# Layer 0 of a four-layer network: the second expert stage in four groups of one batch, where two batches shared a group

## The chip, the cores and the metric

The kernel runs on one core of one Trainium2 chip. Its engines are TensorE (PE; its weight loads are shown apart as PEld), VectorE (DVE), ScalarE (ACT), GpSimd (POOL) and SyncE (SP), which here only starts transfers. Each works through its own list of instructions in order and waits for the others by semaphores. The metric is the device time of one execution in microseconds; the median of three runs is 3132.94 us (3131.44 to 3135.03).

## The reference, cut to what matters

The activations `x` are 4 batches of 1024 tokens of 128 channels here. Each layer is a "macaron": half a feed-forward network, an attention, and half the feed-forward network again, each on a layer norm of `x`, each added to `x`:

```
x = x + 0.5 * _L0_ffn_ref(_layernorm(x), ...)      # n = 0 in the kernel
x = x + _L0_attn_ref(_layernorm(x), ...)           # "middle"
x = x + 0.5 * _L0_ffn_ref(_layernorm(x), ...)      # n = 1 in the kernel: the change is here
x = x + 0.5 * _L1_ffn_ref(_layernorm(x), ...)      # "last"
...
```

Layer 0's feed-forward network is a mixture of experts. A router picks 2 of 8 experts for every token and weighs them by a softmax of the two logits; each expert is `gelu(x @ w1.T + b1) @ w2.T + b2` with 512 hidden units:

```
top_vals, top_idx = jax.lax.top_k(logits, K)
probs = jax.nn.softmax(top_vals, axis=-1)
for e in range(E):
    w = jnp.sum(jnp.where(top_idx == e, probs, 0.0), axis=-1)
    h = jax.nn.gelu(jnp.einsum('td,fd->tf', xf, w1[e]) + b1[e], approximate=False)
    y = jnp.einsum('tf,df->td', h, w2[e]) + b2[e]
    out = out + w[:, None] * y
```

Layer 0's attention is over the 16 heads within one token (a 16 x 16 table for every token, 8 channels a head), so a batch's attention needs only that batch's `x`, and so does everything else in the layer. Layers 1 to 3 follow; nothing of them is changed.

## The kernel before, in words

`x` stays in SBUF with channels as partitions, one tile of 128 x 1024 for each batch (`self.X`). A token tile is 128 tokens, so a batch has 8.

Layer 0 is a set of tasks, each a Python generator that writes instructions and yields a planned cost from time to time:

- `route{n}{b}` (`route`, L290 to L428) for expert stage n and a group of batches named by its first, b. It norms the batches, writes their rows to DRAM (L307), takes the top two of the logits, counts the tokens of each expert and gives every token-and-expert pair a slot. Slots come in blocks of 128 of one expert. Its results are tables: `g_source` (which row fills a slot, L416), `g_target` (where a slot's result goes, L419), `g_expert` (each block's expert, L389), `g_p1`, `g_p2` (the weights). Most of it is short VectorE instructions.
- `experts{n}{b}` (`experts`, L430 on), over the group's blocks. For each: SP loads the expert's whole weights `e_w` (L450, a ring of 5 buffers, 578 KB each); POOL gathers 128 rows into `e_xg` (L452); PE transposes them (L456) and VectorE copies them to `e_x` (L458); 4 matmuls up with Gelu on ACT into `e_h` (L466); 4 matmuls down; VectorE adds the bias into `e_y` (L477); POOL scatters the rows to DRAM, `res` (L478). Three blocks are in flight, in different steps.
- `combine{n}{b}` (`combine`, L488 on) for one batch: SP reads the two results of each token back, `c_y` (L503), ACT and VectorE weigh and add them (L508, L509), PE transposes, VectorE adds half of it to `x` (L251).
- `middle{b}` (`l0_attn`, L517 on): layer 0's attention of a batch, 8 token tiles. A tile is mostly four long VectorE instructions of about 2.3 us (two products, L544 and L561, and two sums, L546 and L563), and ends with the product at L564. After four tiles, `x` gets the result (L588); the second L588 ends the task.
- `last{b}` (`l1_ffn`): layer 1's first half feed-forward network of a batch.

How many blocks a group has is fixed by its size, whatever the tokens choose: `blocks_of(tiles)` is (256 x tiles + 8 x 127) // 128, the slots that are needed if every expert's last block is nearly empty. That is 23 for one batch (8 tiles) and 39 for two (16 tiles).

`lanes` (its planner) writes the tasks' instructions down. It keeps a planned clock for every lane and always goes on with the lane whose clock is least; a task starts once the tasks that it names as its predecessors are written. Layer 0 has four lanes: all experts in turn, all combines in turn, a lane with the first stage's routing, the four attentions and the four `last`, and a lane with the second stage's routing. The Tile framework then gives each engine its order, from that order of writing.

The tables of a routing exist once for each mark (`bufs=1`):

```
one = lambda shape, tag, dtype=F32: self.t(wp, shape, tag + mark, dtype, bufs=1)
```

so that a routing with the same mark as an earlier one must wait for the earlier one's last reader. In the kernel before, the second stage has the groups (0, 1), (2,) and (3,), with the marks `_0`, `_1` and `_2`. The routing of (0, 1), `route10`, names `middle0`, `middle1` and `combine03` as its predecessors.

Of the kernel before, what the change touches and what calls it, by code (L numbers as in the profile page):

```python
# [18 lines left out]
B, S, D = 4, 1024, 128  # L19
# [188 lines left out]
class Macaron:  # L208
# [1040 lines left out]
    def layer0(self, moe, m, right, enter, ffn):  # L1249
        m["wqkvc"] = self.centered(m["wqkv"], 3 * D)  # L1250
        pa, pf = enter(right, "l0a"), enter(right, "l1f0")
        side, main = self.side, self.main

        def more(route):
            attn = lambda b, *after: (f"middle{b}", after, lambda: self.l0_attn(side, pa, m, b))
            last = lambda b, ps: (f"last{b}", (f"combine1{b}",), ffn(pf, ps, b))
            return (
                [
                    route(0, (0,), ps=main), route(0, (1,)), route(0, (2, 3)),
                    *[attn(b, f"combine0{b}") for b in range(B)],  # L1260
                    last(0, side), last(1, side), last(2, side), last(3, main),
                ],
                [route(1, (0, 1), "middle0", "middle1", "combine03"), route(1, (2,), "middle2"), route(1, (3,), "middle3")],
            )


        groups = [(0,), (1,), (2, 3)], [(0, 1), (2,), (3,)]
        marks = {(0, (0,)): "_1", (0, (1,)): "_2", (0, (2, 3)): "_0", (1, (0, 1)): "_0", (1, (2,)): "_1", (1, (3,)): "_2"}
        self.macaron("l0", moe, AF.Gelu, groups, marks, more)

    def layer2(self, moe, m, right, enter, ffn):
# [118 lines left out]
```

## Time and profile before

| | us |
|---|---|
| median of three runs | 3132.94 (3131.44 to 3135.03) |
| the profiled execution | 3239.76 |
| its span | 3237.5 |
| layer 0, up to the end of `last3` | 928 |

| share of the span busy | PE | PEld | VectorE | ACT | POOL |
|---|---|---|---|---|---|
| whole kernel | 85% | 49% | 57% | 50% | 25% |

The profiled execution is the one that all lines of the profile come from; it takes longer than the timed runs. Layer 0 lies in the first twelve of the page's 40 slices (each 81 us). In a line of a group or of the timeline, L and a number is the line of the kernel, then come the operation and "out<-in" by the program's names; "[0.30 <-PE bank L456]" is idle time of the engine before that instruction, and who ended it. A table of stretches gives the busy time of each engine in each stretch with its number of instructions, then the granted TensorE clock (1.00 is full), the mean busy share of the DMA engines and the GB/s that they moved.

In the trace of before, the second stage's gathers start at 493.9 us (`experts10`), about 656 us (`experts12`) and 783.4 us (`experts13`); the first stage's last scatter is issued at 377.1 us. The attentions end at 305.5, 421.7, 572.8 and 733.8 us.

### The profile page before, as it was taken

The numbers are of one execution on the slowest core, as the hardware profiler recorded it, in microseconds if no ns is written. First come the engines' busy times: TensorE is split into PE (matmuls) and PEld (weight loads), VectorE is DVE, ScalarE is ACT, GpSimd is POOL, SyncE is SP. The second block draws the span as 40 slices with busy tenths as digits, with TensorE's granted clock in tenths as the row PEclk, the third lists the DMA queues.
The fourth block names the chain that finished last, engine by engine and source line by source line (L and its number), as shares of the span: only waits on it lengthen the run. The fifth ranks groups of instructions, "written<-read, shape, count | busy, mean of one in ns | idle before, by whom it ended". The sixth has DMA issues, their size and how long they took to land. (4 is left out here: it accounts for less than half of the span.)

```text
span 3237.5 us, 47507 instructions
## 1 busy us (share of the span) xinstructions
PE 2766.3 (85%) x17694; PEld 1584.7 (49%) x17694; DVE 1834.3 (57%) x3214; ACT 1626.5 (50%) x3631; POOL 799.3 (25%) x748
## 2 busy tenths in 40 slices
PE   5877537778969999999999999987988976899997
PEld 4666415665633333333333333567877865334333
DVE  3476986774226676676677673452565622354764
ACT  3555524657712565566465666444453544345342
POOL 3566306552440000000000000046434463010110
PEclk8889758889977999999999999989998988788997
DMA  6656415563500000000000000057665675000000
GB/s 211 208 169 196 125 50 160 159 188 119 154 19 9 5 6 4 6 5 6 20 6 4 3 1 1 21 166 233 198 186 163 209 228 162 0 1 1 7 7 13
DMA packets 122886, 277.57 MB, mean 86 GB/s; under 512 B 18016, under 2 KB 67296, under 8 KB 122528
## 3 DMA queue, kind: packets, MB, share of 16 engines
q1 hardware_dynamic: 101792, 231.77, 23.7%
q0 software_dynamic: 20864, 42.77, 4.5%
q8 instruction: 140, 2.29, 0.3%
q14 instruction: 90, 0.74, 0.1%
HBM read 238.43 MB, written 31.85 MB: 83 GB/s over the span
## 5 line engine op out<-in xcount | busy, mean ns | idle before, releaser
L736 DVE TENSOR_REDUCE nm<-two 128x2 f32<-128x1024 f32 x512 | 626.6, 1224 | 290.8 <-PE s L229 271.4
L759 ACT ACTIVATE e<-s 128x512 f32<-128x512 f32 x1024 | 555.8, 595 | 408.7 <-PE s L229 405.7
L466 ACT ACTIVATE e_h<-bank,e_w 128x128 f32<-128x128 f32 x1304 | 451.0, 367 | 495.3 <-PE bank L229 382.9
L229 PE MATMUL bank<-e_x,e_w 128*128 128x128 f32 x2608 | 543.6, 312 | 127.9 <-ACT e_h L466 65.7
L229 PE MATMUL s<-qm,kz 32*128 32x512 f32 x2048 | 635.7, 645 | 0.8 <-ACT e L759 0.8
L229 PE MATMUL two<-kz,qz 32*128 32x512 f32 x2048 | 595.0, 666 | 21.4 <-POOL va L724 2.5
L452 POOL DMA_INDIRECT e_xg<-rows,g_source x326 | 331.6, 1017 | 822.1 <-DVE g_target L419 356.1
L229 PE MATMUL bank<-e_w,e_h 128*128 128x128 f32 x2608 | 475.5, 298 | 56.7 <-ACT e_h L466 31.3
L229 PEld LDWEIGHTS bank<-e_x,e_w 128*128 128x128 f32 x2608 | 413.4, 205 | 219.9 <-ACT e_h L466 113.1
L478 POOL DMA_INDIRECT res<-e_y,g_target x326 | 368.6, 1131 | 300.1 <-DVE e_y L477 135.4
L229 PEld LDWEIGHTS bank<-e_w,e_h 128*128 128x128 f32 x2608 | 387.6, 206 | 89.8 <-ACT e_h L466 46.6
L229 PE MATMUL o<-e,va 128*32 128x256 f32 x4096 | 329.2, 393 | 0.1
L229 PEld LDWEIGHTS two<-kz,qz 32*128 32x128 f32 x2048 | 160.1, 189 | 240.5 <-issue 163.3
L229 PEld LDWEIGHTS o<-e,va 128*32 128x32 f32 x4096 | 81.0, 108 | 391.8 <-issue 371.8
L458 DVE COPY e_x<-bank 128x128 f32<-128x128 f32 x326 | 92.7, 285 | 263.7 <-PE bank L456 139.7
L477 DVE TENSOR_TENSOR e_y<-bank,e_w 128x128 f32<-128x128 f32 x326 | 93.6, 287 | 213.9 <-PE bank L229 191.0
L229 PEld LDWEIGHTS s<-qm,kz 32*128 32x128 f32 x2048 | 207.0, 184 | 10.9 <-issue 7.8
L724 POOL COPY va<-vd 128x256 f32<-128x256 f32 x16 | 6.7, 431 | 626.2 <-PE o L229 537.9
L1131 POOL TENSOR_TENSOR z<-st,r 128x512 f32<-128x512 f32 x32 | 46.2, 1444 | 417.5 <-DVE st L1124 240.2
L456 PE MATMUL bank<-c,e_xg 128*128 128x128 f32 x326 | 97.0, 300 | 39.7 <-DMA e_xg<-rows,g_source 36.2
L466 ACT ACT_TABLE_LOAD x53 | 68.0, 1283 | 24.0 <-PE bank L229 18.0
L544 DVE TENSOR_TENSOR prod<-qkv 128x2048 f32<-128x2048 f32 x32 | 73.1, 2286 | 5.5 <-ACT qkv L536 5.5
(304 smaller groups left out, 3489.0 us busy)
## 6 DMA issues: line engine op xcount, KB each, us to landing
e_w<-in_l0m_dram SPq DMA_DIRECT2D x170, 578.0 KB
e_w<-in_l2m_dram SPq DMA_DIRECT2D x156, 578.0 KB
c_y<-res SPq DMA_DIRECT2D x32, 512.0 KB
rows<-g_xt SPq DMA_DIRECT2D x16, 512.0 KB
e_xg<-rows,g_source POOLq DMA_INDIRECT x326
res<-e_y,g_target POOLq DMA_INDIRECT x326
x<-in_x_dram SPq DMA_DIRECT2D x4, 512.0 KB
qz<-qd SPq DMA_DIRECT2D x64, 32.0 KB
```

Source lines behind the costliest of these rows:

```text
L229: self.nc.tensor.matmul(out, lhsT, rhs, start=start, stop=stop)
L452: nc.gpsimd.indirect_dma_start(out=xg, out_offset=None, in_=rows[:, :], in_offset=at(source[:, k : k + 1]))
L456: nc.tensor.transpose(tp, xg, self.c0["ident"])
L458: nc.vector.tensor_copy(x, tp)
L466: nc.scalar.activation(h[:, fc, :], o[:, fc, :], func, bias=w[:, 2 * FC * P + fc : 2 * FC * P + fc + 1])
L477: nc.vector.tensor_tensor(y, o, w[:, MOE_W - D :], ALU.add)
L478: ins = nc.gpsimd.indirect_dma_start(out=res[:, :], out_offset=at(target[:, k : k + 1]), in_=y, in_offset=None)
L544: v.tensor_tensor(pr, q.unsqueeze(2).to_broadcast(sh), k.unsqueeze(1).to_broadcast(sh), ALU.mult)
L724: nc.gpsimd.tensor_copy(va[n % RING][:, :, :, 1 : 1 + HD], dense[b, "vd"][:, :, 32 * g4 : 32 * g4 + 32].rearrange("p t (h d) -> p t h d", ...
L736: v.tensor_reduce(nm[:, it, h, 2 * pair : 2 * pair + 2], s, AX.X, ALU.max, negate=True)
L759: nc.scalar.activation(es[g], s, AF.Exp, scale=scale)
L1131: (pool if i else v).tensor_tensor(z, st[:, 0:HALF], r, ALU.mult)
```

## The change: one batch to a group in the second stage

The second stage's groups become (0,), (1,), (2,) and (3,). There is one routing for each batch, `route10` to `route13`, and each names only its own batch's attention as its predecessor. Only the marks `_1` and `_2` serve the groups of one batch, in turn: `route12` has the mark of `route10`, `route13` that of `route11`. The first stage's groups (0,), (1,) and (2, 3) and the marks that they had stay.

```diff
-                [route(1, (0, 1), "middle0", "middle1", "combine03"), route(1, (2,), "middle2"), route(1, (3,), "middle3")],
+                [route(1, (b,), f"middle{b}") for b in range(B)],
             )
...
-        groups = [(0,), (1,), (2, 3)], [(0, 1), (2,), (3,)]
-        marks = {(0, (0,)): "_1", (0, (1,)): "_2", (0, (2, 3)): "_0", (1, (0, 1)): "_0", (1, (2,)): "_1", (1, (3,)): "_2"}
+
+        groups = [(0,), (1,), (2, 3)], [(b,) for b in range(B)]
+        marks = {(0, (2, 3)): "_0", **{(n, (b,)): f"_{1 + b % 2}" for n in range(2) for b in range(B)}}
         self.macaron("l0", moe, AF.Gelu, groups, marks, more)
```

## The prediction

> **What bounds the kernel now.** I read the chain of work that ended last first: it is followed back only to 2723 us, so it shows the last layer alone and says nothing of layer 0, where the diff is. Layer 1's attention opens its pools after `last3`, the last task of layer 0 (its first memset starts at 928.14 us), so a shift of layer 0's end shifts everything behind it; the built programs have the same instructions in the same order from there on. So layer 0 is read by itself, first in the slices of the page and the waits up to 1060 us:
>
> ```profile
> DVE  3476986774226676676677673452565622354764
> POOL 3566306552440000000000000046434463010110
> ```
> ```profile
> POOL e_xg L452 <- DVE g_source L416: 115.8, 1, 115.8
> ```
>
> There is a hole: GpSimd (all gathers and scatters of the experts) rests for 115.8 us, in one wait, for `g_source` of `route10`. It looks like the thing to win. But VectorE (DVE) is at 9 in those slices: it computes attention. Next, busy time by stretches, cut at the second X addition of each batch's attention (L588), in the order middle1, middle2, middle3, then route13, experts13 and the tail:
>
> ```profile
> core 0: us, PE busy (x) PEld busy (x) DVE busy (x) ACT busy (x) POOL busy (x), PEclk, DMA share, GB/s
> 305.50:421.70 116.20, 65.62 (x384) 52.08 (x383) 97.67 (x132) 54.87 (x128) 41.08 (x31) 0.77 0.38 113
> 421.70:572.80 151.10, 85.66 (x460) 66.45 (x459) 110.00 (x177) 60.73 (x169) 57.22 (x47) 0.73 0.38 120
> 572.80:733.80 161.00, 120.12 (x698) 99.14 (x699) 115.48 (x218) 96.24 (x232) 80.61 (x69) 0.85 0.58 174
> 733.80:783.40 49.60, 43.27 (x243) 29.31 (x241) 25.73 (x90) 43.96 (x83) 7.82 (x9) 1.00 0.39 121
> 783.40:887.60 104.20, 92.54 (x523) 69.51 (x523) 31.32 (x79) 70.50 (x138) 43.68 (x46) 0.93 0.49 143
> 887.60:928.10 40.50, 29.28 (x81) 15.63 (x82) 11.15 (x22) 10.05 (x19) 0.96 (x1) 0.75 0.10 30
> ...
> 378.00:494.00 116.00, 32.94 (x129) 20.55 (x127) 102.54 (x151) 29.64 (x96) 0.20 (x2) 0.57 0.16 54
> ```
>
> In the hole VectorE is busy 102.5 of 116 us (88%). The chain that ends layer 0 is attention by attention: middle1, middle2, middle3, then batch 3's routing, its experts, its combine, its last ffn: 116.2 + 151.1 + 161.0 + 194.3 us from 305.5 to 928.1. Experts of other batches matter only as far as they delay that chain. How much, the timeline of VectorE tells, by the end of each attention tile (columns: start, length, engine, line, form):
>
> ```profile
> 346.78 0.28 DVE L564 TENSOR_TENSOR o<-o,sm 128x128 f32<-128x128 f32 x1
> 359.81 0.28 DVE L564 TENSOR_TENSOR o<-o,sm 128x128 f32<-128x128 f32 x1
> ...
> 388.76 0.28 DVE L564 TENSOR_TENSOR o<-o,sm 128x128 f32<-128x128 f32 x1
> 400.20 0.28 DVE L564 TENSOR_TENSOR o<-o,sm 128x128 f32<-128x128 f32 x1
> ```
>
> A tile beside some four expert blocks takes 13.0 us, a tile with none 11.4. The step to the first tile of a next batch is far dearer, because norm, projection and table reloads go round PE, ACT and DVE: from L588 at 572.79 to the first L564 at 602.62 is 29.8 us.
>
> **The change part by part.**
>
> *More blocks.* A group of 16 tiles has 39 blocks, two of 8 have 23 each: 7 more blocks (170 to 177). Each is a 578 KB weight load on SP's queue, a gather and a scatter on POOL's (1.0 and 1.1 us), 9 PE operations, 4 ACT (0.367 each), 2 DVE (0.287 each).
>
> *One more routing.* 52 VectorE instructions and 13.6 us busy for one batch (sum of the lines 304 to 427 of `route12`), 19.8 us and 59 for the pair. Three of one batch, before middle3 ends, in place of a pair and one: 40.8 - 33.4 = +7.4 us. The rows DMA count stays four; `g_expert` is read for 7 blocks more.
>
> *Experts moved forward.* In the built program's order, POOL's first gather of `experts10` now stands ahead of nine of the last scatters of `experts02`, where it stood behind them all. The hole is filled. Between the ends of middle0 and middle3 VectorE's order has 595 instructions for 525: routing 156 for 111, experts 174 for 148. The 26 expert instructions are 7.4 us, with the routing +14.8: DVE busy goes from 323.2 us (the three rows) to 338.
>
> *middle1: 116.2 becomes 161.* Its order with routing, experts and combines is, row for row on DVE, PE and ACT, that of middle3 before the change (the same counts of expert instructions done at its start, 41 of 78). So I take the row of middle3: **+44.8 us**. Floor 150 (without its worst waits), ceiling 170 (one more weight wait).
>
> *middle2: 151.1 becomes 142.5.* By pieces, each from the interval nearest in its counts: first tile with 12 routing instructions 29.8; second tile with 29 of them 23.3 (24.8 less five expert instructions); third with combine10 and the first blocks of `experts11` 18 (13.5, plus 3.5 for the combine, plus a wait for the first gather); fourth 14; first X addition 6.8; then 9, 15, 13.7, 9.5 and 3.4 with almost no experts behind the last. **-8.6 us.**
>
> *middle3: 161.0 becomes 153.* Here a new wait: `experts11` ends with middle2, and `combine11` stands next on DVE, ACT and PE, ahead of middle3's norm. It waits for the last scatter and the reload of `c_y`. The end of layer 0 has the same thing: last `e_y` at 887.02, second X addition at 900.02, 13 us. I take 12, then 27 for the first tile (421.72 to 448.23 was 26.5, with no experts either), 12.5 and 19 with the routing, 13, 4.6, 11.3, 17.9, 14.4, 11.2 and 10 (the tiles of middle2 before). **-8 us.** Behind that wait also stands the rows write of `route12` and all weight loads of `experts12` on SP, inside the same 12 us.
>
> *Tail: 194.3 becomes 183.* Before, `experts12` still drains beside `route13`, and ACT is busy 44.0 of 49.6 us. After, it is gone from there: 23 activations and 13 table loads fewer (20 loads become 7). Instead `combine12` stands in front, again some 10 us on ACT. So routing's logits come at about +18 (before: 754.0 - 733.8 = 20), the rest takes 13.5 us of its own, 6 + 1.4 for ffn instructions between and 2 to 3 of waits: `g_source` at +41 for +48.7. `experts13` loses combine12's 3.9 us of VectorE. **-11 us** (bounds 0 and -25, the latter if the routing runs as `route00` did, in 15 us).
>
> *Table loads.* The Trainium skill speaks against mixing: "ScalarE: Activation LUTs", section "What ACT_TABLE_LOAD costs", prices each change of function set at 1283 ns and a drain of 1380 more, 2.66 us. This trace agrees on the load and shows no drain:
>
> ```profile
> 743.15 1.28 ACT L466 ACT_TABLE_LOAD   x1
> 744.45 0.37 ACT L466 ACTIVATE e_h<-bank,e_w 128x128 f32<-128x128 f32 x1
> ```
>
> The change adds 11 loads in the four middles and takes 13 from the tail. By the row that is +14 and -17 us of ACT, by the page +29 and -35. I take the row, and only the tail's on the path: in the middles ACT has room (96.2 of 161 us in the fullest), and middle1's loads are in the row that I copied. If that cover were gone, up to 14 us more.
>
> *Shared buffers.* Every group now uses marks `_1` and `_2`, so `route12` overwrites the tables of `route10`, `route13` those of `route11`. Their last readers (the combines) stand ahead on the same engines; nothing waits, provided the scatters end as above.
>
> **Sum:** 44.8 - 8.6 - 8 - 11 = **+17 us** on the profiled execution, 3239.8 (span 3237.5, 2.3 around it). That execution is 3.4% above the median of the runs shown, 3132.9; scaled by 0.967 it is +17: about **3150 us**.
>
> **The rivals.**
>
> *A, faster: the hole's pace everywhere.* VectorE kept 88% in the hole, and the skill's "Perfetto Trace Analysis", section "Optimization Strategy", says that interleaving stretches with different bounds may help. If 0.88 held over all three middles, 338/0.88 = 384 us for 428: -44, with the tail -55, times 0.967: 3080 us. By the rows where the two are already interleaved the share is 0.73 and 0.72. It decides at 338 us in 428 + 11, a share of 0.77: above about 0.78 the change pays by over 0.2%. Chance 0.14.
>
> *B, no difference.* middle2 and middle3 run at their floor: eight tiles at 11.3, 20 for the start, 13.6 of routing, 13 of experts, 140 each. That is -15 against mine: +2, 3135 us. Chance 0.14.
>
> *C, clearly slower.* All three go at middle3's share of 0.717: 338/0.717 = 471, +43, tail -11: +32, 3164 us; with a full wait for weights at each of the two additional group starts (3.1 us a load, three loads) up to 3184. Chance 0.17.
>
> *D, the likeliest: as summed.* Chance 0.55, its own range 3139 to 3162.
>
> **How the numbers follow.** 0.2%, 6.3 us, is about what a measurement tells from no change. Slower: D and C, 0.72; same 0.14 (B); faster 0.14 (A). The range reaches from 3126, into A's partial forms, to 3184, C's end; it leaves out A's full form and little else.
>
> **What would show it.** middle1 (L588 to L588 on VectorE) near 161 us, where it was 116; no single gather wait of over 60 us on POOL; middle3's start held by `c_y` for some 10 us; the stretch from middle3's end to `g_source` near 41 us with ACT far less busy; 177 weight loads of layer 0. It is wrong if VectorE stays above 78% busy from 305 us to middle3's end, or if middle2 and middle3 take more than 160 us each.

## The result

The changed kernel takes 3141.94 us (median of 8 runs, 3139.77 to 3146.66), the kernel before beside it 3129.41 (8 runs, 3123.61 to 3135.03): a ratio of 1.0041, 95% interval 1.0031 to 1.0050, or **+12.5 us**. It is slower by about 0.4%. The prediction said 3150, +17 on the median of before, and slower with 0.72.

The runs were made in several sessions, in which the kernel before took 3129 to 3130 us (the result; e9 to e11) or 3246 to 3251 us (e1 to e4; e5 to e8; e12), and the chip of e1 to e4 gave the other pace in e9 to e11, so comparisons are made inside one session unless the text says otherwise. Stages are compared with e5 and e6, the two kernels profiled in one session: their middle0 ended at 304.7 and 305.7 us, that of the prediction's profile at 305.5.

The profile of the changed kernel that was taken with the result, the slices of VectorE and GpSimd:

```profile
DVE  3586868684326676676677675262566631445764
POOL 4665546062340000000000000027444573000110
```

The hole of GpSimd seems filled, but a hole stands one stage later, slice 8. The waits of GpSimd up to 1060 us in the same profile (engine and line, the releaser, then us in total, times, longest):

```profile
POOL e_xg L452 <- DVE g_far L417: 97.9, 2, 62.3
...
POOL e_xg L452 <- DVE frstd L272: 43.8, 1, 43.8
```

Before there was one gather wait of 115.8 us; now there are three, of 62.3, 35.6 (97.9 - 62.3) and 43.8 us, one at the first gather of each of the last three groups. The hole was cut in pieces more than filled; the pieces sum to 141.7 us.

Stretches of the changed kernel in the run e6, cut as the prediction cut those of before: middle1, middle2, middle3, `route13`, `experts13`, the rest of layer 0.

```profile
core 0: us, PE busy (x) PEld busy (x) DVE busy (x) ACT busy (x) POOL busy (x), PEclk, DMA share, GB/s
305.70:464.30 158.60, 118.99 (x695) 98.58 (x694) 115.31 (x218) 95.68 (x231) 79.24 (x69) 0.84 0.59 176
464.30:610.50 146.20, 103.92 (x594) 85.94 (x595) 109.04 (x195) 84.14 (x199) 64.55 (x53) 0.80 0.48 144
610.50:755.60 145.10, 82.12 (x486) 64.97 (x486) 106.97 (x184) 63.48 (x164) 55.88 (x46) 0.76 0.41 126
755.60:802.00 46.40, 34.61 (x142) 20.86 (x140) 25.70 (x85) 20.69 (x52) 1.61 (x2) 0.82 0.30 101
802.00:898.40 96.40, 91.29 (x515) 67.50 (x515) 27.91 (x72) 69.26 (x131) 43.55 (x45) 0.96 0.48 141
898.40:941.00 42.60, 30.71 (x80) 16.47 (x80) 11.47 (x24) 10.05 (x19) 1.10 (x3) 0.72 0.09 28
```

middle1 has nearly the counts of before's middle3 on every engine, as the prediction had it (695 PE instructions beside 698, 218 on VectorE in both), and takes nearly its time: 158.6 us for 161.0.

| us, by the second L588 of each attention; the tail is from there to the end of layer 0 | middle1 | middle2 | middle3 | tail | sum |
|---|---|---|---|---|---|
| before (e5) | 118.8 | 150.1 | 160.9 | 195.5 | 625.3 |
| after (e6) | 158.6 | 146.2 | 145.1 | 185.4 | 635.3 |
| measured change | +39.8 | -3.9 | -15.8 | -10.1 | +10.0 |
| predicted change | +44.8 | -8.6 | -8 | -11 | +17 |

### The profile page after: what moved, and what is told of

It reads as the page before. It is cut to its first block, busy times and chain, and to the rows that moved or that the text cites. A ratio compares the mean times of both kernels' runs of the same rounds, so it can differ in the third digit from the quotient of the medians.

```text
span 3141.0 us, 47923 instructions
## 1 busy us (share of the span) xinstructions
PE 2747.0 (87%) x17817; PEld 1586.9 (51%) x17817; DVE 1840.3 (59%) x3272; ACT 1631.5 (52%) x3658; POOL 814.3 (26%) x762
## 5 line engine op out<-in xcount | busy, mean ns | idle before, releaser
L466 ACT ACTIVATE e_h<-bank,e_w 128x128 f32<-128x128 f32 x1332 | 459.8, 368 | 410.6 <-PE bank L229 396.4
L452 POOL DMA_INDIRECT e_xg<-rows,g_source x333 | 344.1, 1033 | 760.1 <-DVE g_target L419 340.0
L229 PEld LDWEIGHTS bank<-e_x,e_w 128*128 128x128 f32 x2664 | 420.8, 204 | 167.6 <-ACT e_h L466 111.6
L229 PEld LDWEIGHTS two<-kz,qz 32*128 32x128 f32 x2048 | 159.4, 189 | 240.2 <-issue 163.8
L229 PEld LDWEIGHTS s<-qm,kz 32*128 32x128 f32 x2048 | 206.9, 183 | 11.3 <-issue 7.8
L1131 POOL TENSOR_TENSOR z<-st,r 128x512 f32<-128x512 f32 x32 | 46.2, 1445 | 419.2 <-DVE st L1124 240.2
L512 PE MATMUL bank<-c,c_y 128*128 128x128 f32 x128 | 35.7, 381 | 52.5 <-DVE c_y L509 51.9
L508 ACT ACTIVATE c_y<-c_y,g_p 128x128 f32<-128x128 f32 x128 | 40.7, 388 | 72.0 <-DMA c_y<-res 72.0
```

Source lines behind the costliest of these rows:

```text
L229: self.nc.tensor.matmul(out, lhsT, rhs, start=start, stop=stop)
L452: nc.gpsimd.indirect_dma_start(out=xg, out_offset=None, in_=rows[:, :], in_offset=at(source[:, k : k + 1]))
L466: nc.scalar.activation(h[:, fc, :], o[:, fc, :], func, bias=w[:, 2 * FC * P + fc : 2 * FC * P + fc + 1])
L508: nc.scalar.mul(y[0][:, i, :], y[0][:, i, :], plan["p1"][:, n * NT + i, :])
L1131: (pool if i else v).tensor_tensor(z, st[:, 0:HALF], r, ALU.mult)
```

## The experiments

The theory at the start was that of the prediction: attention by attention is the chain, the early start fills middle1 with other work, and the later stretches give back less than it costs. The rival that grew out of the prediction's own list was the padding: seven more blocks, whose price on the path the prediction had never named. The table gathers what the runs gave. "Late" is the number of VectorE instructions of experts (`e_x`, `e_y`; two a block) that ran after middle3's end, "within" those between the ends of middle0 and middle3. The four columns behind them are steps in us. The ratio is that of the timed runs; it can differ by some us from the difference of the medians, and both are given where they do. The profiled executions are single ones: behind layer 0, where all these kernels have the same instructions, they differ by up to 10 us (2304.5 in e1, 2315.0 in e8), so the profiles are compared by the steps in layer 0 and not by their totals.

| run | blocks in stage 2 | within | late | middle1 | middle2 | middle3 | tail | ratio to before, 95% |
|---|---|---|---|---|---|---|---|---|
| e1 before | 85 | 148 | 59 | 118.5 | 151.2 | 164.0 | 196.3 | 1.0000 (0.9982 to 1.0018) |
| e2 before, 7 empty blocks more | 92 | 153 | 68 | 120.8 | 152.9 | 162.9 | 212.2 | 1.0078 (1.0048 to 1.0109) |
| e3 four groups, late start | 92 | 152 | 69 | 119.0 | 155.6 | 158.8 | 213.2 | 1.0063 (1.0039 to 1.0088) |
| e4 groups (0), (1, 2), (3) | 85 | 124 | 83 | 161.9 | 102.7 | 149.3 | 229.6 | 1.0054 (1.0040 to 1.0069) |
| e5 before | 85 | 148 | 59 | 118.8 | 150.1 | 160.9 | 195.5 | one run |
| e6 after | 92 | 174 | 47 | 158.6 | 146.2 | 145.1 | 185.4 | 1.0042 (1.0028 to 1.0056) |
| e7 after, 85 blocks | 85 | 162 | 45 | 156.2 | 149.6 | 125.9 | 181.7 | 0.9936 (0.9912 to 0.9960) |
| e8 after, one combine later | 92 | 174 | 47 | 161.0 | 143.0 | 139.0 | 186.8 | 1.0003 (0.9987 to 1.0019) |
| e9 before, less attention | 85 | 148 | 59 | 99.5 | 131.4 | 132.3 | 191.6 | 0.9787 (0.9761 to 0.9812) |
| e10 after, less attention | 92 | 174 | 47 | 131.6 | 124.5 | 133.5 | 178.5 | 0.9835 (0.9809 to 0.9860) |
| e11 after, two combines later | 92 | 174 | 47 | 150.0 | 142.3 | 136.6 | 170.2 | 0.9984 (0.9974 to 0.9993) |
| e12 e11, closing product first | 92 | 178 | 49 | 159.4 | 153.6 | 137.8 | 175.7 | 0.9967 (0.9952 to 0.9981) |

e1 to e4 share a session, e5 to e8 the next, e9 to e11 the third; e12 stands alone.

**e1: the kernel before once more**, unedited.

> The kernel before, unchanged, for a second profile of it: the first one's execution was 3.4% longer than the median of its runs, and its attention of batch 0, the same instructions in both kernels, ended at 305.5 us where the changed kernel's ended at 278.4. Theory (attention chain on VectorE): this profile has middle0's end near 278, the same hole of some 105 to 115 us on POOL, middle1 near 110, middle2 near 140, middle3 near 150, and a tail near 185; total 1.000 of before. Rival (the first profile was representative): middle0 ends near 305 again.

3248.58 us against 3247.94 for the same kernel beside it, and nearly the steps of the first profile, with middle0's end at 313.2 us. The rival holds: the first profile was no odd execution.

**e2: the blocks without the regrouping.**

```diff
-        blocks = blocks_of(gt)
+        blocks = blocks_of(gt) + out["more"]
...
-            return plans.setdefault((n, group), {"mark": marks[n, group]})
+            return plans.setdefault((n, group), {"mark": marks[n, group], "more": {("l0", 1, (0, 1)): 7}.get((name, n, group), 0)})
```

The same is added where `experts` counts its blocks, and the two constant tables that are as long as the blocks grow with them (not shown).

> Before, with 46 blocks in the group of two in place of 39: the seven more blocks alone, without the third routing and without the earlier start. They hold no token, but load, multiply and scatter as others do. Theory 1 (attention chain plus what is added to it): seven blocks are 4 us of VectorE in middle3, and leave experts12 with some 5 blocks more beside route13, where ACT is nearly full: +8 us (0.2 to 0.4%). Theory 2 (the padding is the whole cost): +12 us or more. Theory 3 (the moving of the experts is the cost, blocks are hidden): +0 to +3.

+25 us by the ratio (1.0078), +23 by the medians: three times what the prediction's theory expected, and on the padding's side. By the steps of the two profiles it is +19. The three middles hardly felt it (+2.3, +1.7, -1.1 against e1); the tail went from 196.3 to 212.2. All expert blocks form one lane. Seven more in its middle push back everything behind them, and the lane ends with layer 0. The stretches of e2 in its tail, `route13` and then all the rest:

```profile
745.00:791.00 46.00, 40.76 (x224) 27.21 (x224) 23.33 (x84) 41.76 (x81) 10.77 (x11) 1.00 0.45 127
791.00:957.30 166.30, 138.75 (x707) 101.03 (x706) 46.82 (x118) 94.52 (x184) 51.05 (x53) 0.89 0.41 119
```

`route13` is as quick as ever; the stretch behind it is 166.3 us, where e1 has 943.2 - 795.7 = 147.5. That is where the leftover of `experts12` runs.

**e3: four groups, but as late as before.**

```diff
-                [route(1, (b,), f"middle{b}") for b in range(B)],
+                [route(1, (0,), "middle0", "middle1", "combine03"), *[route(1, (b,), f"middle{b}") for b in range(1, B)]],
```

> Groups of one batch as in the changed kernel, but route10 waits for middle1 and combine03 as before: blocks and routing of the change without its earlier start. Theory 1: the hole is back, middle1 near 110, but middle3 carries more experts and experts12 is left with 23 expert instructions on VectorE (11 blocks) beside route13: +20 to +28 us against before, some 10 slower than the changed kernel. Theory 3 (the early start itself is what costs): +0 to +6, faster than the changed kernel. Theory 2: +12, as the changed kernel.

+20 us by the ratio (1.0063), +19 by the medians: at the foot of the first theory's span, and by its stages nearly e2, with a tail of 213.2 for 212.2. Four routings where e2 has three make no visible difference; the seven blocks do. Against the change as it is (+0.42%) the early start is worth about 7 us by the ratios, whose intervals overlap, and 11 us by the steps (646.7 us in sum from middle0's end, 635.3 in e6, of the next session).

**e4: the early start without additional blocks or routing.**

```diff
-        groups = [(0,), (1,), (2, 3)], [(0, 1), (2,), (3,)]
+        groups = [(0,), (1,), (2, 3)], [(0,), (1, 2), (3,)]
```

with the routing of (1, 2) behind `middle1`, `middle2` and `combine03`, and its own mark `_0` (not shown).

> Second stage in groups (0,), (1, 2), (3,): 85 blocks and three routings as before, but route10 starts after middle0 as in the changed kernel. The early start without any added work. Theory 1: middle1 as in the changed kernel (near 150), a hole in middle2 instead, and 18 blocks of the pair are left beside route13 and ahead of experts13: +30 us. Theory 2 (padding alone): 0. Theory 3 (the early start costs): +10 to +15, from middle1.

+18 us by the ratio (1.0054), +14 by the medians: at or just above the third theory's span, and far under the first's. It does not say that an early start is bad: GpSimd now waited 136.3 us in one piece for the pair's `g_source`, after the first group was done. middle2 fell to 102.7 us, freed of the experts, and 83 late instructions made the tail 229.6. Its middle1, 161.9, is within a microsecond of the prediction's 161, for the same written order.

**e5 and e6: both kernels in one session.** e5 is before unedited, e6 the change.

> The kernel before once more, so that its stages and those of the changed kernel come from one chip. On the chip of the runs so far it takes 3248 us, with steps of 118.5, 151.2 and 164.0 us from the end of middle0 to the ends of middle1, middle2 and middle3, and 196.3 us from there to the end of layer 0. Theory 1 (chips differ in a common factor): whatever the chip, the four steps stand to each other as these do, within 3 us after scaling by the end of middle0 (313 us there). Rival (the chip changes which wait decides): one of the steps differs by over 6 us after that scaling.

> The changed kernel on the same chip as the kernel before. Theory 1 (the sum of the prediction with its terms): middle1 +40 to +45 us against the kernel before, middle2 -2 to -9, middle3 -8 to -18, the tail from middle3's end -8 to -16; in all +8 to +17, ratio 1.003 to 1.005. Rival (the trace of the changed kernel, from a faster chip, is a picture of that chip alone): middle1 less than +36 and the other three together no better than -24.

e5's steps are those of e1 within 3.2 us as they stand; scaled by the end of middle0, as was expected, they are up to 4.5 us apart, over the theory's 3 and under the rival's 6. e6's are in the first theory's spans (middle1's +39.8 just under its lower edge). They are the table of the section on the result.

**e7: the change with the blocks of before.** 21, 21, 21 and 22 blocks in the four groups, by the edit of e2 with other numbers:

```diff
-            return plans.setdefault((n, group), {"mark": marks[n, group]})
+            return plans.setdefault((n, group), {"mark": marks[n, group], "more": {("l0", 1, (0,)): -2, ("l0", 1, (1,)): -2, ("l0", 1, (2,)): -2, ("l0", 1, (3,)): -1}.get((name, n, group), 0)})
```

> The changed kernel with 21, 21, 21 and 22 expert blocks in the four groups instead of 23 each, so 85 in all, as many as the kernel before; the last blocks of each group, which are mostly or wholly empty, are left out. Theory 1 (the seven blocks are the smaller part: the earlier ends of middle2 and middle3 and the additional routing make the rest): 6 to 12 us less than the changed kernel, so still 0 to +6 above the kernel before. Theory 2 (a block costs what it did when seven were added to the kernel before, 25 us for seven): 20 to 28 us less than the changed kernel, so some 8 to 15 us below the kernel before. Theory 3 (the blocks are hidden): within 3 us of the changed kernel.

3231.05 us: 31.6 less than the change by the medians (20 less by the ends of layer 0 in the two profiles, of which e6's is of an execution 8.7 us under its median), and **20 below the kernel before**. The second theory holds: the gain is at the lower edge of its 20 to 28 us by the profiles, above the upper one by the medians. With equal blocks the regrouping wins 0.64%; the seven blocks cost more than that. By stage, most of it is middle3, 145.1 to 125.9. Part of that is a wait that only moved: with two blocks fewer, `combine11` falls before middle2's last addition. VectorE in e7 there (start, length, engine, line, form, and the idle time before it with its releaser):

```profile
609.06 1.93 DVE L509 SCALAR_TENSOR_TENSOR c_y<-c_y,g_p,c_y 128x128 f32<-128x128 f32 x7 [8.24 <-DMA c_y<-res]
613.27 0.69 DVE L588 TENSOR_TENSOR x<-x,bank 128x512 f32<-128x512 f32 x1 [1.42 <-PE bank L229]
637.88 0.29 DVE L564 TENSOR_TENSOR o<-o,sm 128x128 f32<-128x128 f32 x1
```

The 8.24 us for `c_y` are still paid, in middle2 (whose close took 12.7 us for e6's 4.2), and middle3's first tile then takes 24.6 for 37.0. So the move gives some 4 us; the rest, some 16 by the ends of layer 0, I put down to the shorter lane of experts, which no run separates from it. This is no version to keep: the 23 blocks of a group are what the worst distribution of tokens needs, and fewer hold only for tokens like these.

**e8: combine11 away from middle3's head.**

```diff
-                yield f"combine{n}{b}", (f"experts{n}{group[0]}",), lambda b=b: self.combine(side, wp, group, b, plan(n, group))
+                late = ("route12",) if (name, n, b) == ("l0", 1, 1) else ()
+                yield f"combine{n}{b}", (f"experts{n}{group[0]}", *late), lambda b=b: self.combine(side, wp, group, b, plan(n, group))
```

> The changed kernel, with the combine of batch 1 held back until the routing of batch 2 is written, so that it no longer stands ahead of middle3's start. Theory 1 (the new wait at middle3's start, for the results read back, is on the path with about 10 us): 8 to 12 us less than the changed kernel, the step of middle3 shorter by as much. Rival 1 (the wait takes the place of another that is as long, of middle3's own projection or of the routing): within 3 us. Rival 2 (the combine stands in the way of middle3's tiles further on as much as at its start): middle3 the same or up to 5 us longer.

3252.18 us, 10.5 less than the change and level with before. The head of middle3 on VectorE in the change, e6:

```profile
610.51 0.69 DVE L588 TENSOR_TENSOR x<-x,bank 128x512 f32<-128x512 f32 x1 [1.51 <-PE bank L229]
...
620.20 1.93 DVE L509 SCALAR_TENSOR_TENSOR c_y<-c_y,g_p,c_y 128x128 f32<-128x128 f32 x7 [8.23 <-ACT c_y L508]
...
629.15 0.20 DVE L272 RECIPROCAL arstd<-astd 128x8 f32<-128x8 f32 x1 [3.85 <-ACT astd L270]
...
647.49 0.28 DVE L564 TENSOR_TENSOR o<-o,sm 128x128 f32<-128x128 f32 x1
```

and in e8:

```profile
614.65 0.69 DVE L588 TENSOR_TENSOR x<-x,bank 128x512 f32<-128x512 f32 x1 [1.51 <-PE bank L229]
...
620.40 0.20 DVE L272 RECIPROCAL arstd<-astd 128x8 f32<-128x8 f32 x1 [3.93 <-ACT astd L270]
...
638.73 0.28 DVE L564 TENSOR_TENSOR o<-o,sm 128x128 f32<-128x128 f32 x1
```

From the end of middle2 to the norm's reciprocal: 18.6 us in e6, 5.8 in e8; to the end of the first tile 37.0 and 24.1. The line of e6 with L509 says ACT, which itself waits for what SP reads back. SP's waits in e6, from 590 to 660 us:

```profile
SPq L307 <- ACT g_xt L306: 20.4, 1, 20.4
SPq L503 <- DMA res<-e_y,g_target: 18.3, 1, 18.3
```

The read of `c_y` stood 18.3 us on SP for the last scatter. Behind it in the queue stood the rows write of `route12`, which then waited 20.4 us more for its own `g_xt`; so the queue itself is not shown to have cost anything. What the combine held up is middle3's norm, behind it on the engines. Of the 12.8 us won at the head, middle3 kept 6.1 by the profile (its fourth tile, where the combine now lies, went from 11.3 to 19.4), and the four steps together 5.5; the timed runs have 10.5. So the wait is on the path, as the first theory says, and a part of it is paid again in the tile that takes the combine, as the second rival says.

**e9 and e10: is VectorE's own work on the path?** The same edit in both kernels leaves out the second product of attention; the sum behind it reads the first product `pr`, which is handed on to it (not shown):

```diff
-            pv = self.t(wp, sh, "prod", bufs=3)
-            v.tensor_tensor(pv, ex.unsqueeze(2).to_broadcast(sh), values.unsqueeze(1).to_broadcast(sh), ALU.mult)
+            pv = pr.rearrange("p h t d -> p (h t d)").rearrange("p (h d t) -> p h d t", h=NH, d=HD)
```

> The kernel before without the second product of layer 0's attention, the line that takes 2.27 us of VectorE in each of 32 token tiles (18.1 us a batch, 72.5 us in all); the sum behind it reads the first product, so the attention computes something else. Theory 1 (VectorE's own work sets the pace of every stretch of attention): 60 to 72 us less than the kernel before, 16 to 18 in each of the four attentions. Theory 2 (it does so only where attention runs nearly alone, as in middle1, and elsewhere the expert blocks' round through TensorE, ScalarE and VectorE sets it): middle1 shorter by 16 to 18 us, middle2 and middle3 by 5 to 12 each, in all 35 to 55.

> The changed kernel without the same product. Theory 1: as much less than the changed kernel as the kernel before lost, within 6 us. Theory 2: middle1, now full of expert blocks, is shorter by only 5 to 12 us where it was by 16 to 18 in the kernel before, so the changed kernel loses 6 to 12 us less than the kernel before and the distance between the two grows from about +12 to +18 or more.

Before lost 69.5 us (3130.33 to 3060.81). After lost about 66: the change itself was not run beside e10, but the result's ratio 1.0041 on 3130.33 makes 3143.2, an estimate, and e10 took 3076.83. The first theory holds, and the second falls. The middles in the profile of after that came with the result and in that of e10 (columns as above; from two sessions in which before took 3129 and 3130 us):

```profile
278.40:428.40 150.00, 115.09 (x698) 96.30 (x697) 115.13 (x218) 96.05 (x231) 79.56 (x71) 0.87 0.63 185
428.40:570.60 142.20, 100.60 (x595) 83.68 (x594) 108.86 (x196) 83.73 (x198) 64.44 (x54) 0.81 0.49 151
570.60:713.80 143.20, 82.31 (x485) 65.43 (x484) 106.51 (x184) 63.78 (x164) 56.73 (x46) 0.76 0.42 128
```
```profile
260.10:391.70 131.60, 107.58 (x698) 90.14 (x697) 97.46 (x210) 94.80 (x231) 78.45 (x72) 0.94 0.69 208
391.70:516.20 124.50, 92.28 (x598) 76.90 (x596) 91.17 (x188) 83.09 (x199) 59.16 (x54) 0.88 0.57 175
516.20:649.60 133.40, 76.80 (x481) 62.35 (x480) 89.65 (x175) 63.46 (x163) 48.48 (x46) 0.78 0.43 137
```

middle1, full of expert blocks and with VectorE at 77%, shortened by 18.4 us for 115.13 - 97.46 = 17.7 us of VectorE taken out. middle2 gave 17.7 for 17.7. A busy share below one did not mean here that the engine's work was covered: the waits came in addition to it. TensorE's busy time fell as well (115.09 to 107.58 us in middle1, at a clock of 0.94 for 0.87), and what share of the gain that is was not separated. middle3 gave only 9.8 for 16.9, so a part of it is held by something else than attention's products.

**e11: both waits moved.**

```diff
-                yield f"combine{n}{b}", (f"experts{n}{group[0]}",), lambda b=b: self.combine(side, wp, group, b, plan(n, group))
+                late = (f"route1{b + 1}",) if (name, n) == ("l0", 1) and b in (1, 2) else ()
+                yield f"combine{n}{b}", (f"experts{n}{group[0]}", *late), lambda b=b: self.combine(side, wp, group, b, plan(n, group))
```

> The changed kernel, with the combine of batch 1 held back until the routing of batch 2 is written and the combine of batch 2 until the routing of batch 3 is. Nothing is left out. Theory 1 (each of the two combines waits for its results read back at the head of a stretch, and each wait is on the path): the first gives the 10 us that holding back batch 1's alone gave, the second 5 to 8 more in the tail, since routing 3 then starts some 8 us earlier: 14 to 18 us less than the changed kernel, so 2 to 6 us below the kernel before. Rival (the tail is set by the experts of batch 3 and their results, and the combine of batch 2 then delays these by as much): the tail within 3 us of the changed kernel's, in all 8 to 12 us less.

3124.17 against 3130.33: 6.2 below before, and about 19 below the change (3143.2, the estimate of above), a little over the theory's 14 to 18. Both kernels are beaten, by little. The tail in the profile of after that came with the result, `route13` and the rest:

```profile
713.80:759.40 45.60, 34.02 (x142) 20.46 (x140) 25.78 (x85) 20.71 (x52) 1.63 (x2) 0.85 0.31 103
759.40:892.00 132.60, 117.90 (x595) 81.84 (x595) 39.52 (x95) 79.60 (x150) 44.71 (x46) 0.91 0.37 112
```

and in e11:

```profile
705.10:736.80 31.70, 28.79 (x134) 16.99 (x133) 23.45 (x83) 20.26 (x52) 1.68 (x2) 1.00 0.44 148
736.80:875.30 138.50, 123.16 (x603) 84.84 (x603) 40.74 (x97) 79.80 (x151) 44.80 (x46) 0.89 0.36 107
```

The start of `route13` on VectorE in after, whose middle3 ends at 713.79 us:

```profile
723.28 1.93 DVE L509 SCALAR_TENSOR_TENSOR c_y<-c_y,g_p,c_y 128x128 f32<-128x128 f32 x7 [6.98 <-ACT c_y L508]
...
732.65 0.20 DVE L272 RECIPROCAL frstd<-fstd 128x8 f32<-128x8 f32 x1 [2.04 <-ACT fstd L270]
```

and in e11, whose middle3 ends at 705.13:

```profile
710.88 0.20 DVE L272 RECIPROCAL frstd<-fstd 128x8 f32<-128x8 f32 x1 [2.04 <-ACT fstd L270]
```

Batch 3's norm comes 5.8 us after middle3 for 18.9, and `route13` takes 31.7 us for 45.6, so `combine12` had held it up by 13.9; the work that it moved costs 5.9 later on. Net 8.0 in the tail and 6.6 in middle3.

**e12: the closing product ahead of the blocks.** On top of e11, the last pause of the planner in an attention (11.2 of its units, room for some four blocks) comes after the closing product instead of before it.

```diff
-            yield 11.2
+            if i + 1 < NT:
+                yield 11.2
             if k == 3:
...
                 v.tensor_tensor(X[:, c], X[:, c], y, ALU.add)
+        yield 11.2
```

> The changed kernel with both combines held back as in the run before, and with each attention's last product and its addition to x written before the expert blocks that so far stood between them and the last token tile (five blocks' instructions behind middle1's last tile, four behind middle3's, none behind middle2's). Nothing is left out. Theory 1 (blocks that stand ahead of an attention's closing product on TensorE cost their full pace there, some 2.1 us each, and cost less at the next attention's start, where VectorE and TensorE wait anyway): middle0 and middle1 each 6 to 9 us shorter from the last tile to the closing addition, middle3 4 us, of which the next attention's first tile gives back a third to a half; in all 6 to 14 us less than the run before, so 12 to 20 us below the kernel before. Rival (the blocks cost the same wherever they stand on TensorE, so the next first tile is longer by what the close is shorter): within 3 us of the run before.

0.9967 of before (0.9952 to 0.9981), 10.8 us below. Against e11's 0.9984 (0.9974 to 0.9993) the intervals overlap, so it is not shown that it adds anything. The close of middle1 and the next first tile in e6, of another session, which has the blocks where e11 has them (the last tile of middle1, its closing addition, the first tile of middle2):

```profile
447.54 0.28 DVE L564 TENSOR_TENSOR o<-o,sm 128x128 f32<-128x128 f32 x1
464.29 0.69 DVE L588 TENSOR_TENSOR x<-x,bank 128x512 f32<-128x512 f32 x1 [2.27 <-PE bank L229]
493.72 0.28 DVE L564 TENSOR_TENSOR o<-o,sm 128x128 f32<-128x128 f32 x1
```

and in e12, where L589 is the closing addition:

```profile
451.30 0.28 DVE L564 TENSOR_TENSOR o<-o,sm 128x128 f32<-128x128 f32 x1
457.21 0.69 DVE L589 TENSOR_TENSOR x<-x,bank 128x512 f32<-128x512 f32 x1 [3.07 <-PE bank L229]
497.50 0.28 DVE L564 TENSOR_TENSOR o<-o,sm 128x128 f32<-128x128 f32 x1
```

The close fell from 16.8 us to 5.9, and the tile behind it rose from 29.4 to 40.3: the sum is 46.2 in both (46.6 in e8, which has e6's order). There the rival holds: five blocks cost the same on either side of this seam. middle3's close is 3.7 us for 7.6 in e8 and in e11; whether the tail pays that back is not shown, since no run with e11's tail stands beside e12.

**A theory that the runs make together.** In e1 to e8 the sum of the three middles and the tail go roughly with the number of expert blocks in them. Each line here is drawn through two runs, e4 and e6, and tried on others. The tail: 185.4 us with 47 late instructions (e6), 229.6 with 83 (e4), which is 44.2/36 = 1.23 an instruction, 2.5 us a block; that line gives 200.2, 211.2, 212.4 and 182.9 for e5, e2, e3 and e7, measured 195.5, 212.2, 213.2 and 181.7. The middles: 413.9 us with 124 (e4), 449.9 with 174 (e6), 0.72 an instruction, 1.4 us a block; it gives 431.2, 434.8 and 434.1 for e5, e2 and e3, measured 429.8, 436.6 and 433.4, but 441.3 for e7, measured 431.7, and 449.9 for e8, measured 443.0: the two in which `combine11` has left middle3's head fall below it. So a block beside attention still costs 1.4 of 2.5 us: by these lines some four tenths of it are hidden, and no more. The change carries 13 blocks more in the middles and 6 fewer in the tail: 13 x 1.44 - 6 x 2.46 = +4 us by these lines, measured +10. What the lines do not hold (up to 10 us) I put down to where single waits such as that for `c_y` fall; that part is argued.

## Why the prediction was right, and where its sizes were off

**The chain.** That layer 0 is read attention by attention, then the tail, fits these runs: the stage sums give +10.0, and +11.0 with middle0's end, which came 1.0 us later in e6 with the same instructions up to there; timed in that session it is +11.7 by the medians. Against the +17 the terms were off by -5.0, +4.7, -7.8 and +0.9 us. That the first two cancel is luck, and so is the size of the tail, as told below; what remains is middle3. None of the signs of being wrong came: VectorE stayed under 78%, and middle2 and middle3 under 160 us. The 177 weight loads were there.

**middle1, 161.** Measured 158.6 (e6), 161.9 (e4), 161.0 (e8). Copying the row of a stretch with the same order of instructions was the best step of the prediction. In the profile that came with the result it was 150.0, the floor that was given.

**middle2, 142.5.** Measured 146.2; the gain was 3.9 and not 8.6. The pieces: first tile 29.4 (29.8 said), second 21.4 (23.3), third 19.4 (18), fourth 13.8 (14), first addition 5.6 (6.8), then 10.5, 15.9, 13.7, 12.3 and 4.2 for 9, 15, 13.7, 9.5 and 3.4. Of the 3.7 us too many, 2.8 are in the last tile; no piece was off by over 3 us.

**middle3, 153.** The new wait was found ahead of time and sized right: wait and first tile were 37.0 us for 12 + 27, and e8 divides them into 12.8 and 24.1. That it was on the path, e8 showed. The miss, 145.1 for 153, is in the wait and the first tile (2.0), the fourth tile (11.3 for 13) and the late pieces: 15.2, 16.9, 8.5 and 8.0 us for 17.9, 14.4, 11.2 and 10. The figures for these came from before's middle2, and not because that held more work: its tiles of 17.9 and 11.2 us have 18 and 12 VectorE instructions, 9 and 7 of them of experts, and so have those of 15.2 and 8.5 in e6. The same counts took 2.7 us less in a new place; why is open.

**The tail, 183.** Measured 185.4, but the path to it was not the one given. ACT was relieved as said (20.7 us busy for 43.9 in e5, and up to `g_source` 6 table loads for 19), and `g_source` came only 2.6 us earlier (46.4 for 49.0), where the prediction put it at +41. The routing's logits, which it put at +18, came at +25.3, later than before (+22.0 in e5); only from there to `g_source` did the routing gain, 21.3 us for 27.2. The step that failed is the one from "23 activations and 13 table loads fewer" to "`g_source` at +41 for +48.7": it let the relief of ACT through to the routing and gave the `combine12` in front "some 10 us on ACT". e11 shows that this combine held the routing by 13.9 us, which ate most of the relief. That the tail still came out near 183 is luck. The rest of the gain, 146.5 to 139.0 us, is the stretch of `experts13`, with fewer blocks left over in the tail (47 late instructions for 59) and, as the prediction had it, without combine12's VectorE work.

**More blocks.** This is the term that was mis-sized. The prediction counted what seven blocks hold (PE operations, activations, 7.4 us of VectorE with the earlier ones) and put no price on them by themselves. Its own lines would have priced a block beside attention at (13.0 - 11.4) / 4.5, some 0.35 us, for the four and a half blocks in the tile that it showed; the lines of above have 1.4. On the path seven blocks cost 19 us (e2) and some 16 to 20 us (e7) by the profiles, 2.3 to 2.9 us each, and 23 to 32 us by the timed runs, more than the whole loss in either way. The sign came out right, I think, because the copied row of middle3 and the counted tail held that price without naming it. Whether the 11 table loads more in the middles cost anything was not tried by itself.

**VectorE sets the pace.** Right, and stronger than put: in e10 a microsecond off VectorE went with a microsecond off middle1 and middle2. It does not hold for every microsecond: the fourth routing of e3 (VectorE 327.4 us busy in the middles, 324.4 in e2) did not show in the steps. VectorE's busy time in the middles rose by 7.8 us, from 323.5 in e5 to 331.3 in e6, half of the 14.8 that was summed from single instructions: their records overlap in part. Its share from middle0's end to middle3's was 331.3/449.9 = 0.74, under the 0.77 from which rival A decides. Rival B's floor of 140 a stretch was not reached by middle2 and middle3 (146 and 145 us; 142 and 143 in the profile that came with the result).

**"No single gather wait of over 60 us."** Missed: 62.3. From about middle2's end on GpSimd rested until `route12` was done, since `experts11` ended with middle2 and the next group must wait for the next routing. The prediction had both facts in the steps of middle3 and did not put them together.

## What to carry to other kernels

Splitting work with a worst-case padding has to be priced by the blocks that it adds, at what a block costs where nothing hides it and at what it costs beside the bound engine, both read off the trace, before anything is said about an earlier start. A long wait on an idle engine is no gain to be had until one asks what the engine would then do to the chain: here filling it put blocks into attention that was on the path, and the wait came back in three pieces. In queues that run in order, look at who stands at the head when a stage changes: moving two small tasks that waited for a transfer gave back about 19 us and turned the loss of 12.5 us into a gain of 6.

## What the runs showed of the hardware

- A load of ScalarE's function table takes 1.283 us, every one of the 190 in the profile of e6, the next activation starts 0.01 us after its end, and the load itself 0.02 us after the activation before it (both medians). No other cost of a change of function is seen there.
- A block of experts has two VectorE instructions of 0.29 us, and cost 1.4 us beside attention and 2.5 us in the tail, by the lines through e4 and e6.
- An engine that is busy for 77% of a stretch can still set its length: 17.7 us less work on VectorE went with 18.4 us less in middle1 (e10).
- Each engine takes its list in order, so a small task that waits for a transfer holds what is behind it: in e6 VectorE idled 8.23 us for `c_y`, and middle3's norm came 12.8 us later than in e8, where the same task stood further back.
